# Order of a put-off channel's two products beside the last mixing

## The chip, the cores and the metric

The kernel runs on one core of one Trainium2 chip. The metric is the device time of one execution in microseconds (us); less is better. Before the change the median of three runs is 2989.25 us (2988.33 to 2990.84).

## The reference

The input is x, 4 images of 64 channels of 256 x 256 values in float32. Four layers follow each other.

```python
# layers 0, 1 and 3: a long convolution per channel
k   = einsum('ijk,imk->ijmk', hx, hy)[0]        # rank one per channel: hx along rows, hy along columns
y   = irfft2(rfft2(x, 512x512) * rfft2(k, 512x512))[..., :256, :256]
out = y + x * bias[:, None, None]

# layer 2: a Haar transform, a mixing of channels, and back
f1  = haar2d(x)
for i in range(2):
    f4  = einsum('bchw,oc->bohw', f1 * v[i], conv_w[i])
    acc = acc + sign(f4) * relu(abs(f4) - tau[i])
out = haar2d(acc, inverse=True) + x
```

hx and hy come from small networks with three sines each. The convolution's kernel of a channel is an outer product of one function of the row and one of the column, cut to the first 256 outputs, so the convolution is a product with a triangular Toeplitz matrix from each side.

## The kernel before, in words

**Products.** An image channel lies on chip as `[128, 2, 256]`: 128 partitions, two halves of the rows, 256 columns. One convolution is two products. `contract` (L186) makes one: four matmuls against a Toeplitz tile that was read from DRAM by `toeplitz` (L177). The four matmuls are eight records in the trace, since a float32 matmul is split in two. `first` (L192) makes the first product of a channel into a PSUM bank (`pa`), and ScalarE copies it to an SBUF tile (`a`, L198). `second` (L203) multiplies that tile into another bank (`py`), and VectorE adds bias times the channel's own input and writes the result (`y`, L211). So a channel's second product can't start until ScalarE has copied its first.

**Layers and stages.** For each image b, `convolutions(b)` does layers 0 and 1 and the forward Haar transform, and writes the coefficients to DRAM. `mixing(b)` (L310) then takes them in 64 groups g of four coefficient rows each: `load` (L314), `mix` (four matmuls, L334, into the bank pair `px`; then scaling of `px` to `f4`, ten of sixteen pieces on VectorE, L351, and six on ScalarE, L353, for the last image), `shrink` (abs and sign on ScalarE, L359 and L360, subtraction on VectorE, L361), `signed` (L366) and `add` (L370), which writes the tile `z`. `inverse(b)` (L377) reads `z` channel by channel: after `butterfly` come a copy (L387), row products (L394, L395, bank `pw`), a column product (L407, bank `pu`), the addition of the kept input (L411, L414, L415), giving `u`; then layer 3 with `first`, `second` and the store, which `last` (L430) lists.

**Put-off channels.** For images 0 to 2 every third channel (2, 5, ..., 62: 21 channels, 63 in all) stops at `u`, which goes to DRAM (`late`, L425). `convolution` (L437) takes these 63 up again and does layer 3 for them while the mixing of image 3 runs. Its stages per channel are: `load` (u and the Toeplitz tile through the SP queue, L444 and L180), `first`, `second` and the store (through ScalarE's queue, L434).

**The order.** Nothing is issued when a stage function is defined. `at(tick, place, run, unit)` (L227) collects events, and at the end they are sorted by tick, then place, then order of entry, and run. The mixing of image 3 gives group g, at tick start + g, place -1 to `mix`; -2 to `shrink` of the group before, -3 to `signed` of the one before that, and -4 to `add`. Loads have place 0, two ticks ahead. `convolution` gives each channel a tick; the 63 ticks are spread evenly by `spread` (L451) from start - 2 to two ticks behind the end of the mixing, so that some ticks have no channel. Its four stages get the four ticks from there on, with places 0, -1, -2, -3. `mixing` enters its events first, so at equal places its stage comes first. The framework below (a tile context) then orders the instructions of each engine itself, with this order as priority, gives out the buffers, and sets the waits.

**Buffers at this place.** The channel's u lies in the tag "in" (three buffers) from its load until `y` has been computed. The copy `a` has the tag "mid" (two buffers), the result `y` "co" (two), the Toeplitz tile "toep" (five). The four PSUM banks of tag "mm" take `pa`, `py`, `pw` and `pu`; two pairs of banks of tag "mix" take `px`. `f4` and `mag` have two buffers each.

The functions that the change touches, and what calls them:

Of the kernel before, what the change touches and what calls it, by code (L numbers as in the profile page):

```python
# [37 lines left out]
def conv_seq_kernel(ctx, tc, x, fz, fw, bias, decay, haar, haar_row, factors, vt, taut, wmix, out):  # L38
# [138 lines left out]
    def toeplitz(layer, c, name):  # L177

        t = tp.tile([P, 2, S], F32, name=name, tag="toep")
        nc.sync.dma_start(t, ap(pads[layer], c * 2 * ROW, [[1, P], [ROW, 2], [1, S]]))  # L180
        return t
# [10 lines left out]
    def first(b, st, key, layer, new):  # L192
        def run(c):
            s = st[c]
            ps = bank(f"p{new}_{b}_{c}")
            contract(ps, s[key], s[layer][:, 0, :])
            a = io.tile([P, 2, S], F32, name=f"{new}_{b}_{c}", tag="mid")
            nc.scalar.copy(a, ps)  # L198
            s[new] = a

        return run

    def second(b, st, key, layer, res, new, tag, ahead=None):  # L203
        def run(c):
            s = st[c]
            if ahead is not None:
                s[ahead] = toeplitz(ahead, c, f"t{ahead}_{b}_{c}")
            ps = bank(f"p{new}_{b}_{c}")
            contract(ps, s[key], s[layer][:, 1, :])
            y = io.tile([P, 2, S], F32, name=f"{new}_{b}_{c}", tag=tag, bufs=BUFS[tag])  # L210
            nc.vector.scalar_tensor_tensor(y, s[res], bsb[:, layer, c : c + 1], ps, ALU.mult, ALU.add)  # L211
            s[new] = y

        return run
# [12 lines left out]
    def at(tick, place, run, unit):  # L227
        events.append((tick, place, len(events), run, unit))
# [201 lines left out]
    def last(b, st):  # L430
        return [
            first(b, st, "u", 2, "a3"),
            second(b, st, "a3", 2, "u", "y3", "co"),
            lambda c: nc.scalar.dma_start(out[b, c].rearrange("(k p) w -> p k w", p=P), st.pop(c)["y3"]),  # L434
        ]

    def convolution(which, ticks):  # L437

        for (b, c), tick in zip(which, ticks):
            st = {}  # L440

            def load(c, b=b, st=st):
                u = io.tile([P, 2, S], F32, name=f"v_{b}_{c}", tag="in", bufs=3)
                nc.sync.dma_start(u, late[b, c])  # L444
                st[c] = {"u": u, 2: toeplitz(2, c, f"t2_{b}_{c}")}

            for s, stage in enumerate([load, *last(b, st)]):
                at(tick + s, -s, stage, c)


    def spread(begin, end, n=C):  # L451
# [23 lines left out]
    for b in range(B):  # L475
        mixing(b, start, 12 if b + 1 < B else 6)
        end = start + groups + 3
        if b + 1 < B:
            ready = convolutions(b + 1, spread(ahead, end + 2), in_parts=range(C), border=end)
        else:  # L480
            convolution(
                [(i, c) for i in range(B - 1) for c in sorted(put_off)], spread(start - 2, end + 2, (B - 1) * len(put_off))
            )
        inverse(b, end, put_off if b + 1 < B else ())

        start = max(end + C, ready + 3)
        ahead = start - 3
# [111 lines left out]
```

## Time and profile before

| what | value |
|---|---|
| median of 3 runs | 2989.25 us |
| profiled execution: its time, its span | 2989.2 us, 2987.4 us |
| granted TensorE clock | 1.00 |
| TensorE matmul busy | 2919.9 us (98%) |
| VectorE busy | 2551.9 us (85%) |
| ScalarE busy | 2156.5 us (72%) |
| first and last first product of a put-off channel (start) | 2444.3 us, 2743.5 us |
| first and last result y of a put-off channel (start) | 2450.9 us, 2748.1 us |
| put-off u, issue to landing, min / median / max | 2.6 / 3.7 / 5.8 us |

The profile is of one execution, whose own time is 1.8 us over the span from its first to its last instruction. Engines are PE (matmul), PEld (weight load), DVE (VectorE), ACT (ScalarE), and the queues SP and ACT that issue DMAs. In a timeline each row has its start, its length, the engine, the line of the kernel and the tiles written and read; a bracket tells how long the engine stood idle before it and what ended that. Times of start count from the span's start. Lengths of neighbouring VectorE instructions overlap, so the distance between two starts tells more than the length.

### The profile page before, as it was taken

Reading aid. Unit: us, or ns where it says so; the run is one execution under the profiler, and the core shown is the slowest. Engines: PE = TensorE matmul, PEld = TensorE weight load, DVE = VectorE, ACT = ScalarE, POOL = GpSimd, SP = SyncE. Lnnn points to the kernel's source line nnn. Section 1 sums busy time; section 2 is a strip of 40 time slices with the busy share of each in tenths; the row PEclk is TensorE's granted clock in tenths of the full one; section 3 lists DMA queues with packets and bytes.
Section 4 is the critical chain, followed back from the end, with each engine's and each line's share of the span. In section 5 each row is a group of like instructions: output and inputs, shape, how many; then the busy total and the mean of one; then the engine's idle time right before and its main releaser. Section 6 shows DMA issues by size and latency. Waiting matters only on the chain. (4 is left out here: it accounts for less than half of the span.)

```text
span 2987.4 us, 51999 instructions
## 1 busy us (share of the span) xinstructions
PE 2919.9 (98%) x16950; PEld 2610.5 (87%) x16950; DVE 2551.9 (85%) x4576; ACT 2156.5 (72%) x5005; POOL 0.2 (0%) x4
## 2 busy tenths in 40 slices
PE   7999999999999999999999999999999999999999
PEld 6899988888888888888888988888888988888998
DVE  4766778999998879999989879999998889998776
ACT  1333338999986758989886758989886768887554
POOL 0000000000000000000000000000000000000000
PEclk9999999999999999999999999999999999999999
DMA  4877777766667876676777776676677877777676
GB/s 146 245 234 229 230 231 210 210 200 199 210 201 243 249 219 203 207 209 203 208 213 236 253 224 196 209 211 204 206 211 235 255 238 231 231 232 220 212 210 187
DMA packets 562496, 649.72 MB, mean 217 GB/s; under 512 B 44369, under 2 KB 447412, under 8 KB 562100
## 3 DMA queue, kind: packets, MB, share of 16 engines
q1 hardware_dynamic: 446132, 494.94, 58.0%
q10 hardware_dynamic: 116096, 151.46, 14.2%
q8 instruction: 137, 2.24, 0.3%
q14 instruction: 131, 1.07, 0.1%
HBM read 426.77 MB, written 219.48 MB: 216 GB/s over the span
## 5 line engine op out<-in xcount | busy, mean ns | idle before, releaser
L189 PE MATMUL py<-t,a 128*128 128x256 f32 x3072 | 923.3, 382 | 17.8 <-ACT a L198 8.6
L198 ACT COPY a<-pa 128x512 f32<-128x512 f32 x768 | 473.3, 617 | 442.2 <-PE pa L190 298.2
L190 PEld LDWEIGHTS py<-t,a 128*128 128x128 f32 x3072 | 583.4, 190 | 79.3
L353 ACT ACTIVATE f<-px,vt 128x64 f32<-128x64 f32 x2688 | 589.7, 351 | 75.7 <-DVE f L351 75.3
L190 PE MATMUL py<-t,a 128*128 128x128 f32 x3072 | 590.0, 274 | 0.0
L189 PEld LDWEIGHTS py<-t,a 128*128 128x128 f32 x3072 | 491.6, 191 | 69.5 <-ACT a L198 32.0
L334 PE MATMUL px<-wb,f 128*128 128x256 f32 x2048 | 504.3, 382 | 19.6 <-ACT f L353 19.6
L334 PEld LDWEIGHTS px<-wb,f 128*128 128x128 f32 x2048 | 362.1, 190 | 67.2 <-ACT f L353 32.1
L361 DVE TENSOR_TENSOR mag<-mag,vt 128x1024 f32<-128x1024 f32 x256 | 312.7, 1222 | 18.8 <-ACT mag L359 16.6
L366 DVE SCALAR_TENSOR_TENSOR mag<-mag,f 128x1024 f32<-128x1024 f32 x256 | 312.8, 1222 | 4.4 <-DVE sd L266 0.3
L397 ACT CAST w<-pw 128x512 fp32r<-128x512 f32 x256 | 150.2, 587 | 226.5 <-PE pw L395 214.6
L189 PE MATMUL pa<-t,y 128*128 128x256 f32 x1024 | 306.6, 381 | 2.5 <-DVE y L211 1.6
L189 PE MATMUL pa<-t,x 128*128 128x256 f32 x1024 | 305.6, 380 | 1.5 <-issue 1.5
L359 ACT ACTIVATE mag<-f 128x1024 f32<-128x1024 f32 x256 | 282.9, 1105 | 21.1 <-DVE z L370 7.0
L387 ACT COPY zc<-z 128x512 f32<-128x512 f32 x256 | 282.4, 1104 | 2.3 <-ACT w L397 1.9
L360 ACT ACTIVATE f<-f 128x1024 f32<-128x1024 f32 x256 | 273.2, 1067 | 13.1 <-DVE sd L257 5.7
L278 DVE TENSOR_TENSOR sp<-sd,sp 128x512 fp32r<-128x512 f32 x256 | 176.6, 690 | 92.6 <-ACT sp L277 91.9
L211 DVE SCALAR_TENSOR_TENSOR y<-x,bsb,py 128x512 f32<-128x512 f32 x256 | 191.0, 746 | 55.5 <-PE py L190 48.7
L189 PE MATMUL pa<-t,u 128*128 128x256 f32 x772 | 232.8, 383 | 3.6 <-PE pu L407 3.5
L411 DVE SCALAR_TENSOR_TENSOR t<-r,pu 128x512 f32<-128x512 f32 x256 | 175.0, 684 | 59.4 <-PE pu L407 55.2
L190 PEld LDWEIGHTS pa<-t,x 128*128 128x128 f32 x1024 | 194.6, 190 | 26.3
L190 PEld LDWEIGHTS pa<-t,y 128*128 128x128 f32 x1024 | 194.5, 190 | 26.3
(65 smaller groups left out, 4471.6 us busy)
## 6 DMA issues: line engine op xcount, KB each, us to landing
t<-pad SPq DMA_DIRECT2D x768, 256.0 KB, 4.0
x<-in_x SPq DMA_DIRECT2D x256, 256.0 KB, 3.9
keep<-sd ACTq DMA_DIRECT2D x256, 256.0 KB, 2.9
coef<-co SPq DMA_DIRECT2D x256, 256.0 KB, 3.1
f<-coef SPq DMA_DIRECT2D x256, 256.0 KB, 4.0
r<-keep SPq DMA_DIRECT2D x256, 256.0 KB, 3.2
out_y<-y ACTq DMA_DIRECT2D x256, 256.0 KB, 3.7
late<-u ACTq DMA_DIRECT2D x63, 256.0 KB, 2.8
```

Of the source, the lines that this page charges most:

```text
L189: nc.tensor.matmul(ps[:, m, :], src[:, 0, m * P : (m + 1) * P], t[:, ::-1], start=True, stop=False)
L190: nc.tensor.matmul(ps[:, m, P:], src[:, 1, m * P : (m + 1) * P], t[:, : P - 1 : -1], start=False, stop=True)
L198: nc.scalar.copy(a, ps)
L211: nc.vector.scalar_tensor_tensor(y, s[res], bsb[:, layer, c : c + 1], ps, ALU.mult, ALU.add)
L278: nc.vector.tensor_tensor(w[:, 1], t, w[:, 0].bitcast(F32), ALU.subtract)
L334: nc.tensor.matmul(ps[:, h, q, :], f[:, q, h * P : (h + 1) * P], wb.rearrange("p r n -> p (r n)"), start=True, stop=True,)
L353: nc.scalar.mul(f4[:, j], px[:, j], scale(g, 0)[:, j : j + 1])
L359: nc.scalar.activation(mag, f4, AF.Abs)
L360: nc.scalar.activation(f4, f4, AF.Sign)
L361: nc.vector.tensor_sub(mag, mag, over(g, 1, 16))
L366: nc.vector.scalar_tensor_tensor(mag, mag, 0.0, st[g]["f4"], ALU.max, ALU.mult)
L387: nc.scalar.copy(a, z[:, :, :, c].rearrange("p h (i k) -> p h k i", k=2))
```

## The change

The places of a put-off channel's stages are no longer 0, -1, -2, -3 but 0, -2, -1, -3. `load` and the store keep their places and all four keep their ticks. In a tick, the emitted order of what stands around `mix(g)` was: second(c-2), mix(g), first(c-1). It becomes: first(c-1), mix(g), second(c-2). No instruction, buffer or transfer is added or taken away.

```diff
@@ convolution @@
                 nc.sync.dma_start(u, late[b, c])
                 st[c] = {"u": u, 2: toeplitz(2, c, f"t2_{b}_{c}")}
 
-            for s, stage in enumerate([load, *last(b, st)]):
-                at(tick + s, -s, stage, c)
+
+            for s, (place, stage) in enumerate(zip((0, -2, -1, -3), [load, *last(b, st)])):
+                at(tick + s, place, stage, c)
```

## The prediction

> **What bounds the kernel now.** I began with the busy shares of the page, then went to the stretch that the change touches, from the first put-off product (2444 us) to the first row product of the last inverse (2739 us). The first line says only that TensorE is the engine to watch over the whole span:
>
> ```profile
> PE 2919.9 (98%) x16950; PEld 2610.5 (87%) x16950; DVE 2551.9 (85%) x4576; ACT 2156.5 (72%) x5005; POOL 0.2 (0%) x4
> ```
>
> The view by stretches has, in order: span of the stretch, PE, PEld, DVE, ACT and POOL busy, clock, DMA share, GB/s.
>
> ```profile
> 2640.00:2680.00 40.00, 39.29 (x211) 34.52 (x210) 39.71 (x47) 35.62 (x83) 0.00 (x0) 1.00 0.79 234
> 2680.00:2724.00 44.00, 43.28 (x236) 38.52 (x235) 43.80 (x52) 38.43 (x95) 0.00 (x0) 1.00 0.76 223
> 2724.00:2740.00 16.00, 12.44 (x73) 10.83 (x72) 12.16 (x17) 10.27 (x20) 0.00 (x0) 1.00 0.78 223
> 2740.00:2987.00 247.00, 243.40 (x1557) 224.22 (x1555) 174.75 (x322) 138.78 (x192) 0.00 (x0) 1.00 0.67 203
> ```
>
> See that in the mixing VectorE is as full as TensorE (the six stretches from 2480 to 2724 sum to 242.0 of 244 us). From 2740 on TensorE alone carries the time, one channel each 3.74 us. Only the 16 us between have slack on both.
>
> The timeline of VectorE shows why the order on that engine matters. Two cycles of one group plus one put-off channel (start, us, engine, line):
>
> ```profile
> 2707.00 1.22 DVE L366 SCALAR_TENSOR_TENSOR mag<-mag,f 128x1024 f32<-128x1024 f32 x1
> 2708.14 0.75 DVE L211 SCALAR_TENSOR_TENSOR y<-v,bsb,py 128x512 f32<-128x512 f32 x1
> 2708.80 0.82 DVE L351 TENSOR_TENSOR f<-px,vt 128x640 f32<-128x640 f32 x1
> 2709.53 1.22 DVE L361 TENSOR_TENSOR mag<-mag,vt 128x1024 f32<-128x1024 f32 x1
> 2710.66 0.69 DVE L370 TENSOR_TENSOR z<-mag 128x512 f32<-128x512 f32 x1
> 2711.26 1.22 DVE L366 SCALAR_TENSOR_TENSOR mag<-mag,f 128x1024 f32<-128x1024 f32 x1
> ...
> 2520.45 1.22 DVE L366 SCALAR_TENSOR_TENSOR mag<-mag,f 128x1024 f32<-128x1024 f32 x1
> 2521.78 0.82 DVE L351 TENSOR_TENSOR f<-px,vt 128x640 f32<-128x640 f32 x1
> 2522.52 0.74 DVE L211 SCALAR_TENSOR_TENSOR y<-v,bsb,py 128x512 f32<-128x512 f32 x1
> 2523.17 1.22 DVE L361 TENSOR_TENSOR mag<-mag,vt 128x1024 f32<-128x1024 f32 x1
> 2524.31 0.69 DVE L370 TENSOR_TENSOR z<-mag 128x512 f32<-128x512 f32 x1
> 2524.91 1.22 DVE L366 SCALAR_TENSOR_TENSOR mag<-mag,f 128x1024 f32<-128x1024 f32 x1
> ```
>
> With the channel's result y (L211) straight behind L366 the cycle is 2711.26 - 2707.00 = 4.26 us; with the scaling L351 there it is 2524.91 - 2520.45 = 4.46 us. L351 writes the buffer of f4 (two of them) that L366 has just read, so it starts 1.33 us after L366, where y starts 1.14 us after: 0.19 us lost. Read through from 2480 to 2728, 45 cycles have y straight behind L366 and 2 have L351, then y.
>
> Last, the waits of the matmul stream behind the mixing. Each is a second product (py) standing until the copy (L198) of its own first product is done:
>
> ```profile
> 2726.06 0.70 PE L189 MATMUL py<-t,a 128*128 128x256 f32 x2 [1.54 <-ACT a L198]
> 2729.62 0.70 PE L189 MATMUL py<-t,a 128*128 128x256 f32 x2 [0.67 <-ACT a L198]
> 2733.18 0.70 PE L189 MATMUL py<-t,a 128*128 128x256 f32 x2 [0.67 <-ACT a L198]
> 2736.74 0.70 PE L189 MATMUL py<-t,a 128*128 128x256 f32 x2 [0.67 <-ACT a L198]
> ```
>
> Within the mixing, waits of 2480 to 2724 give:
>
> ```profile
> PEld px L334 <- ACT f L353: 6.7, 12, 1.2
> PE px L334 <- ACT f L353: 4.3, 7, 0.8
> PEld py L189 <- ACT a L198: 4.1, 14, 0.4
> ```
>
> The upper two are back-pressure: TensorE is ahead of the scaling and has no free px.
>
> **What the Trainium skill says.** "Perfetto Trace Analysis", Identifying the Most-Contended Engine: matmul busy time misleads, pipelined PE work looks smaller. So I use start-to-start pitch: a mix is 1.73 us, a product (contract) 1.31 us. "TensorE: Matmul & The Clock Gate", Step-by-step: weights of the next matmul load while the present one runs. The trace agrees: a py that has waited shows 0.70 us for its first pair, others 0.60, so each wait costs 0.10 us more than its gap. "VectorE: DVE Perf Modes", The DRAIN you can't avoid: a next instruction waits for the pipe to empty, unless it is not held. Here instructions of 1.22 us are followed after 1.13 to 1.14 us when independent and after 1.33 when dependent; the measurement decides.
>
> **The change, part by part.** It adds and removes no instruction, byte or buffer; it changes where three stages of a put-off channel stand within a tick. The emitted order is not the engine's order: on TensorE at 2705 I read mix (6 records), py, mix (2), pa. It acts as a rank among ready work. The load and the store keep their ranks (0 and -3), so SP's u and Toeplitz loads and ACT's store keep their place among the mixing's loads and issues. Before: second(c-2), mix(g), first(c-1). After: first(c-1), mix(g), second(c-2). With first go its 4 matmuls (8 records) and ACT's copy, 0.59 us each; ACT has it ahead of mix's six scalings instead of behind. With second go 4 matmuls and VectorE's y, now ranked behind mix's L351.
>
> *TensorE, in the mixing.* Between first(c) and second(c) now stands at least another product or a mix (1.31 or 1.73 us), more than the copy (0.59 us, starting 0.17 us after pa). The 4.1 us of py waits go. But VectorE sets the pace there: group pitch is (2726.71 - 2454.06) / 63 = 4.33 us while TensorE needs 1.73 + 0.89 channels x 2.62 = 4.06. What TensorE gains turns into longer waits at px. Value 0; bounds -2 (VectorE's own stops in that stretch, at most) to 0.
>
> *TensorE, behind the mixing.* The gaps are 1.54 + 3 x 0.67 = 3.55 us; with 4 x 0.10 it is 3.95. If pa of the next channel fills them, 2.7 products come forward from behind 2740, where they cost full price. About 1.4 y of 0.66 us then stand in VectorE ahead of the last z and the butterfly, which release the inverse: 3.55 - 0.9 = -2.6 us. Bounds 0 (nothing ready) and -3.95.
>
> *VectorE.* y now ranks behind L351. Each cycle that turns from the first form to the second costs 0.19 us. If L351 isn't yet free at the end of L366 (its buffer is released only there) and y is ready, y still goes first. I take 8 of the 45: +1.5 us. Bounds 0 and 45 x 0.19 = +8.6.
>
> *Loads of u.* The ring of three "in" buffers is full: u's load at 2704.65 starts as y of 2703.88 ends. The product that uses the load of 2700.39 starts at 2707.04; landing takes 3.7 us (median; 2.6 to 5.8), so 2.95 us are left. Ranked ahead of py and the rest of a mix, pa moves 1.31 + 0.43 us forward: 1.2 us left. A median load stays hidden, the slowest would stand out by 0.9 us. Value 0; upper bound in the rivals. "mid" (2), "toep" (5) and the four product banks hold one channel more between first and second; I find no bound.
>
> *Start of the stretch.* Up to 2480, stops of VectorE sum to 4.6 us, mostly waits for py and px. Reordering may shift these either way: 0, bounds -4 and +2.
>
> **Sum:** -2.6 + 1.5 = -1.1 us against the profiled execution's 2989.2 us (span 2987.4 and 1.8 around it): 2988.1. The median shown is 2989.25, practically the same.
>
> **Rivals.**
> A (the forecast, 0.43): steady part untouched, tail partly recovered: 2988; own range 2984 to 2993.
> B (0.30), slower: y falls behind L351 in nearly all cycles. For it: new rank, and the 4.46 us form already exists. Against: at the end of L366 y was ready and L351 was just being released. 45 x 0.19 - 2.6 = +6.0: 2995; without the tail 2998. It loses from 14 turned cycles on; past 0.2% at 45.
> C (0.12), slower: longer-held u buffers. TensorE stands in order at pa for the load, px behind it is late, VectorE starves. The first 0.28 us per group are covered (4.33 - 4.06 rounded); at a mean wait of 0.5 us it is 63 x 0.22 = +14: 3003. Against: 1.2 us left at the median.
> D (0.15), faster: VectorE's 4.6 us at the start go as well as the tail: -2.6 - 4.6 = -7: 2982. Against: at the start TensorE is full, not waiting.
> That the edit does nothing lies in A.
>
> **How the numbers follow.** 0.2% (6 us) is about what a measurement of this kernel tells from no change. Slower: C and two thirds of B, plus a little of A: 0.33. Faster: D: 0.15. The rest, 0.52, is no change. The range leaves out most of C and the far end of D: 2981 to 3000. A alone would be 2984 to 2993.
>
> **What would show it.** Right: py no longer waits for a; the gaps from 2724 to 2740 shrink from 3.55 to about 1 us; the forms on VectorE stay mostly at 4.26 us. B: cycles at 4.46 us in the many, the first row product near 2748. C: new waits of pa for late or v. Wrong altogether: a change before 2440 us or a longer pitch than 3.74 us behind the mixing.

## The result, and the profile after

The changed kernel is slower: 3008.52 us median of four runs (3003.68 to 3011.66), against 2990.05 us for the kernel before, also of four. The ratio is 1.0062 with a 95% interval of 1.0050 to 1.0074. The forecast was 2988.1 us with a range of 2981 to 3000; the time lies outside it, on the side of rival C.

The profiled execution took 3011.05 us, its span is 3009.24 us, 21.9 us over that of before. Three marks tell where they lie (starts, read from the timelines):

| | last scaling on VectorE (L351) | first row product (L394) | end of span |
|---|---|---|---|
| before | 2726.71 | 2739.46 | 2987.37 |
| after | 2749.29 | 2758.79 | 3009.24 |
| difference in the part | mixing +22.6 | tail 9.50 for 12.75: -3.2 | inverse 250.4 for 247.9: +2.5 |

First the engines of the whole span. PE's busy time has grown by 3 us only, so nearly all of the new time is waiting:

```profile
PE 2923.0 (97%) x16950; PEld 2614.3 (87%) x16950; DVE 2553.6 (85%) x4576; ACT 2158.8 (72%) x5005; POOL 0.2 (0%) x4
```

By stretches (span, PE, PEld, DVE, ACT, POOL busy, clock, DMA share, GB/s), the mixing has lost on both engines. VectorE had 39.7 of 40 us in the first stretch before. In the third row TensorE stands still for most of the time, and its mean clock is 0.61:

```profile
2640.00:2680.00 40.00, 36.41 (x194) 31.93 (x193) 36.64 (x43) 31.90 (x79) 0.00 (x0) 1.00 0.75 214
2680.00:2724.00 44.00, 42.82 (x234) 38.19 (x233) 41.81 (x49) 36.40 (x86) 0.00 (x0) 1.00 0.83 239
2752.00:2762.00 10.00, 3.21 (x12) 2.94 (x13) 6.35 (x10) 6.57 (x11) 0.00 (x0) 0.61 0.27 83
```

The waits from 2480 to 2752 us (who waited, for whom, us in total, times, longest) name the new cause:

```profile
PE pa L189 <- DMA v<-late: 15.7, 18, 2.2
DVE y L211 <- PE py L190: 14.9, 21, 2.4
PEld pa L189 <- PE py L190: 9.6, 15, 1.1
...
PEld px L334 <- ACT f L353: 0.5, 2, 0.3
PEld py L189 <- ACT a L198: 0.3, 1, 0.3
```

The first product (pa) now waits for the load of its u, and VectorE's y for the second product behind it. The wait that the reordering was to remove, py for the copy a, has gone from 4.1 to 0.3 us. The back-pressure at px has gone from 6.7 to 0.5 us as well: TensorE is no longer ahead of VectorE, it is behind.

The chain of waits around 2700 us shows why the load is late (start, us, what):

```profile
2686.45 4.15 DMA v<-late
...
2694.01 0.43 PE py L189 x2
...
2695.36 0.76 DVE y L211
2696.12 0.02 issue
2696.14 3.91 DMA v<-late
2700.05 0.14 issue
2700.18 0.67 PE pa L189 x2
2700.85 1.73 PE px L334 x8
...
2704.76 1.73 PE px L334 x8
2706.49 0.63 PE pa L189 x2
...
2708.66 0.43 PE py L189 x2
2709.09 0.23 PE py L190 x2
2709.33 0.03 issue
2709.35 0.75 DVE y L211
```

and the SP queue's timeline the loads of u in it:

```profile
2690.88 0.32 SPq L444 DMA_DIRECT2D v<-late  x1
...
2696.14 0.32 SPq L444 DMA_DIRECT2D v<-late  x1
...
2700.48 0.32 SPq L444 DMA_DIRECT2D v<-late  x1
...
2705.58 0.32 SPq L444 DMA_DIRECT2D v<-late  x1
...
2710.13 0.32 SPq L444 DMA_DIRECT2D v<-late  x1
```

With three buffers, the load of 2710.13 takes the buffer of the load of 2696.14. One lap is 13.99 us: load and its signal 4.04, the channel's first product with a mix inside it 3.27 (until 2703.45), the second product of the channel in front 1.31, the next mix 1.73, the **next** channel's first product 1.51, the own second product 1.33, y with its signals 0.80. Nothing in this sum is slack. A third of it is 4.66 us per channel, more than VectorE's 4.26. The 40 commonest VectorE cycles of the changed kernel have a mean of 4.76 us.

The chain holds a second loop, and it is as tight. It passes through TensorE's order, not through one buffer. The first product that waits for the load of 2686.45 holds up the second product behind it (2694.01), which is that of the channel in front. Its y (2695.36) frees the buffer for the load of 2696.14. With 2690.88 between them, these are two loads in 9.69 us, or 4.85 us per channel.

The lap in the old order is read from the trace of before:

```profile
2700.39 0.32 SPq L444 DMA_DIRECT2D v<-late  x1
...
2707.04 0.59 PE L189 MATMUL pa<-t,v 128*128 128x256 f32 x2
...
2712.40 0.75 DVE L211 SCALAR_TENSOR_TENSOR y<-v,bsb,py 128x512 f32<-128x512 f32 x1
2713.17 0.32 SPq L444 DMA_DIRECT2D v<-late  x1
```

From load to load that is 12.78 us or three VectorE cycles. With the median landing time of 3.7 us it holds 2.95 us of slack ahead of the first product, and some 1.4 us ahead of y.

The tail, in TensorE's timeline:

```profile
2758.79 0.79 PE L394 MATMUL pw<-hrow,zc 128*128 128x128 f32 x2 [7.38 <-ACT zc L387]
2759.38 0.42 PE L395 MATMUL pw<-hrow,zc 128*128 128x128 f32 x1
2759.59 0.64 PE L394 MATMUL pw<-hrow,zc 128*128 128x128 f32 x2
2760.02 0.42 PE L395 MATMUL pw<-hrow,zc 128*128 128x128 f32 x1
2760.23 1.06 PE L189 MATMUL py<-t,a 128*128 128x256 f32 x2
```

The four waits of before are gone, but one of 7.38 us has come. In TensorE's order the program before has nine products between the last mix and the first row product, the changed one has four (most of the first of them stands behind the mix that it encloses). A second product that is long ready (2760.23) stands behind the row product, which waits for z. The matmuls that follow run at about half speed (0.64 us for what takes 0.39 in the trace of before) until about 2764.

### The profile page after: what moved, and what is told of

Same layout as the page of the kernel before. It is cut to its first block, busy times and chain, and to the rows that moved or that the text cites. A ratio compares the mean times of both kernels' runs of the same rounds, so it can differ in the third digit from the quotient of the medians.

```text
span 3009.2 us, 52033 instructions
## 1 busy us (share of the span) xinstructions
PE 2923.0 (97%) x16950; PEld 2614.3 (87%) x16950; DVE 2553.6 (85%) x4576; ACT 2158.8 (72%) x5005; POOL 0.2 (0%) x4
## 4 chain that ended last, share of the span: by engine, by line
PE 61%; DVE 23%; ACT 6%; DMA 6%; issue 3%; DVEq 0%; ACTq 0%; SPq 0%
PE py L189 15%; PE pa L189 14%; PE py L190 7%; PE pa L190 7%; PE px L334 6%; DVE y L211 5%; DVE mag L366 4%; DVE mag L361 4%; PE pu L407 4%; PE pw L394 4%; ACT f L353 4%; DMA v<-late 2%; DMA keep<-sd 2%; PE pz L285 2%; DVE sd L267 2%
## 5 line engine op out<-in xcount | busy, mean ns | idle before, releaser
L334 PE MATMUL px<-wb,f 128*128 128x256 f32 x2048 | 498.1, 381 | 16.4 <-ACT f L353 16.4
L366 DVE SCALAR_TENSOR_TENSOR mag<-mag,f 128x1024 f32<-128x1024 f32 x256 | 312.4, 1220 | 5.0 <-ACT f L360 0.5
```

Source lines behind the costliest of these rows:

```text
L334: nc.tensor.matmul(ps[:, h, q, :], f[:, q, h * P : (h + 1) * P], wb.rearrange("p r n -> p (r n)"), start=True, stop=True,)
L366: nc.vector.scalar_tensor_tensor(mag, mag, 0.0, st[g]["f4"], ALU.max, ALU.mult)
```

## The experiments

The theory: the new order holds each u for one more channel, so three buffers are too few. The expectations call it the ring theory, a ring being a set of buffers that is used in turn. The rivals: the ranks themselves (the order or rank theory) break the pace of VectorE or of the mix; or the load itself is late, whatever holds the buffer.

**Three slots elsewhere, then four, then eight.** u goes to slots of the tile `sd`, which no other stage uses beside the last mixing, in place of the tag "in". Only the number of slots differs, and the last of the four has the old order.

```diff
-        for (b, c), tick in zip(which, ticks):
+        for i, ((b, c), tick) in enumerate(zip(which, ticks)):
...
-            def load(c, b=b, st=st):
-                u = io.tile([P, 2, S], F32, name=f"v_{b}_{c}", tag="in", bufs=3)
+            def load(c, b=b, st=st, i=i):
+                u = sd[:, i % N].rearrange("p k e w -> p k (e w)")
```

N = 3:

> The new order, the put-off u in three slots of the tile sd, which is idle beside the last mixing, in place of the three buffers of tag 'in'. Ring theory (three buffers for u are too few for the new order): the number is the same, so as slow as the changed kernel, 3004 to 3012 us. If the place in memory or the shared tag matters, it moves by more than 6 us.

Measured 3006.37 us, ratio 1.0059 (1.0044 to 1.0074). As slow as the changed kernel: neither the place nor the shared tag matters. In its waits from 2480 to 2745 stands the same line as above:

```profile
PE pa L189 <- DMA sd<-late: 10.4, 17, 1.5
```

N = 4:

> The new order with four slots. Ring theory: the lap of a buffer in the changed kernel's trace is about 14.0 us, which four slots share as 3.5 us per channel, under the 4.26 us that VectorE needs; the waits of pa for the load go from some 38 us to under 5 and the time to 2984 to 2990 us. Order theory (the ranks themselves break the pace of VectorE or ScalarE, whatever the buffers): within 4 us of the three-slot kernel.

Measured 2986.54 us, 0.9993 (0.9984 to 1.0002). One more slot takes away the whole loss of some 20 us; no wait of pa for a load is left in the list. The 38 us of the expectation was too high: the rows PE and PEld of pa's waits count in part the same time. In the timeline of the changed kernel's TensorE, the gaps ahead of pa (start to start, over the usual distance) sum to 26 us.

N = 8:

> The new order with eight slots. Ring theory: no more than four slots already give, so within 3 us of a_sd4; the copies' two 'mid' buffers limit what is left. If the time falls on by more than 3 us, four slots were still a limit.

Measured 2987.69 us, 0.9994 (0.9985 to 1.0002): no more than four slots give.

N = 8 in the old order:

> The old order with eight slots, the control. Ring theory: in the old order a load landed 2.95 us before its product, so more slots give nothing: 2987 to 2992 us. If more slots help the old order as well, by over 4 us, the ring was a limit of the kernel before and not brought by the change.

Measured 2988.53 us, 1.0000 (0.9991 to 1.0009). The ring was no limit in the kernel before; the edit has made it one.

**Which half of the edit.** Both keep the three buffers.

```diff
-zip((0, -2, -1, -3), [load, *last(b, st)])
+zip((0, -1.5, -2, -3), [load, *last(b, st)])    # o_first_up: second, first, mix
+zip((0, -0.5, -1, -3), [load, *last(b, st)])    # o_second_down: mix, second, first
```

> One half of the edit alone, with the three 'in' buffers: first(c-1) ahead of mix(g), second(c-2) still ahead of first(c-1). Ring theory: u is held no longer than before, since no other channel's product stands between its own two for longer, so 2984 to 2993 us. Rank theory (products ahead of the mix starve VectorE): 3000 us or more.

Measured 2984.79 us, 0.9989 (0.9982 to 0.9996).

> The other half alone, with the three 'in' buffers: second(c-2) behind mix(g), but still ahead of first(c-1). Ring theory: as before, 2984 to 2993 us. Rank theory (y behind L351, or the second product too late): 3000 us or more.

Measured 2985.62 us, 0.9995 (0.9986 to 1.0003).

Each half by itself costs nothing; the first is even a little faster than the kernel before, by 3 us. So it isn't the rank of a product against the mix. It is the crossing of the two halves: only where first(c-1) stands ahead of second(c-2) is u held for one more channel.

**Freeing u early.** The order of the changed kernel and its three "in" buffers, but y takes a slot of `sd`, which doesn't change here, instead of u. This leaves out the own bias term of the 63 channels.

```diff
-    def last(b, st):
+    def last(b, st, res="u"):
...
-            second(b, st, "a3", 2, "u", "y3", "co"),
+            second(b, st, "a3", 2, res, "y3", "co"),
...
-                st[c] = {"u": u, 2: toeplitz(2, c, f"t2_{b}_{c}")}
+                st[c] = {"u": u, "k": sd[:, 0].rearrange("p k e w -> p k (e w)"), 2: toeplitz(2, c, f"t2_{b}_{c}")}
...
-            for s, (place, stage) in enumerate(zip((0, -2, -1, -3), [load, *last(b, st)])):
+            for s, (place, stage) in enumerate(zip((0, -2, -1, -3), [load, *last(b, st, "k")])):
```

> The new order in full with the three 'in' buffers, but the bias term of the 63 put-off channels takes a constant tile in place of u (their own bias term is left out), so u is free after its first product and no longer held until y. Ring theory: the lap falls from some 14 us to load + first product, about 6 us, and the time to that of four slots, 2983 to 2990 us. If it is the load itself or its issue that is late, whatever holds the buffer, it stays over 3000 us.

Measured 2985.53 us, 0.9991 (0.9983 to 1.0000). The same loads, in the same order, with three buffers, are in time once y no longer holds them. This excludes the load's own duration and its issue as the cause.

**Two slots in the old order.** N = 2 in the edit above, in the kernel before.

> The old order with only two slots for u. Ring theory: the least lap of the old order is about load 3.9 + first product 1.3 + part of a mix 1.3 + second product 1.3 + y 0.75 = 8.6 us, so two slots give 4.3 us per channel, just at what VectorE needs: waits of pa for the load appear, and the time rises, but less than in the changed kernel (14.0/3 = 4.7 us): 2990 to 3003 us. If the old order doesn't depend on the slots at all, it stays within 3 us of before.

Measured 3011.30 us, 1.0078 (1.0061 to 1.0095): the same illness without the edit, and more of it than I had expected. The commonest VectorE cycle (33 of them) has a mean of 4.78 us (4.27 to 7.50), so two channels take 9.6 us where I had summed a least lap of 8.6; what makes up the difference was not followed further. The wait is the same:

```profile
PE pa L189 <- DMA sd<-late: 10.9, 13, 2.0
```

**What the four slots leave.** With the ring cured the new order is equal to the old one, not better. Its trace (a_sd4) has the tail's wait in full:

```profile
2738.46 0.80 PE L394 MATMUL pw<-hrow,zc 128*128 128x128 f32 x2 [9.81 <-ACT zc L387]
```

The channels run so far ahead that only the end of one second product, a first and a second are left behind the last mix; they end at 2728.6. Yet one first and two second products still stand behind the first row product. A narrower spread, from four ticks later to three ticks earlier, should bring more products between the two:

```diff
-[(i, c) for i in range(B - 1) for c in sorted(put_off)], spread(start - 2, end + 2, (B - 1) * len(put_off))
+[(i, c) for i in range(B - 1) for c in sorted(put_off)], spread(start + 2, end - 1, (B - 1) * len(put_off))
```

> The new order with four slots, and the 63 ticks spread from start + 2 to end - 1 in place of start - 2 to end + 2, so that three more products stand between the last mix and the first row product. Tail theory (with four slots TensorE stands 10 us at the first row product because the order has put nothing in front of it): that wait falls to about 6 us, no half-clock matmuls follow or fewer, and the time falls from 2986.5 to 2979 to 2984 us. If the mixing gets longer by what the tail saves, it stays at 2985 to 2989 us.

Measured 2982.85 us, 0.9979 (0.9971 to 0.9987): 6 us faster than the kernel before, clear of noise, and the fastest version here. The wait at the first row product is down to 2.45 us, further than expected, and the matmuls behind it are at full speed after their first pair (0.39 us):

```profile
2733.17 0.49 PE L394 MATMUL pw<-hrow,zc 128*128 128x128 f32 x2 [2.45 <-ACT zc L387]
2733.50 0.27 PE L395 MATMUL pw<-hrow,zc 128*128 128x128 f32 x1
2733.61 0.39 PE L394 MATMUL pw<-hrow,zc 128*128 128x128 f32 x2
```

The wait isn't all of the gain, though. By the marks of its trace the mixing is as long as before (274.1 us from the first group's L345 to the last L351; before 274.0). The tail takes 10.94 us for 12.75, the inverse 246.9 for 247.9, with no put-off product left in it. The mixing also starts 4.5 us earlier (2448.1 for 2452.7): the first put-off product now starts at 2458.4, behind that start, where before a first and a second product stood ahead of it. Starts of 2449 to 2453 in other versions with the old spread show that part of this differs from run to run; the shares were not separated.

From 2480 to 2720 us TensorE has no gap left, and a mix starts every 4.35 us, its own work with a channel in every tick (1.73 + 2 x 1.31).

Two controls with the same spread. The old order with its three buffers:

> The old order and three 'in' buffers, with the same later spread, the control for a_sd4_late. If the spread by itself is worth something, 2980 to 2986 us; if a denser row of channels, one in nearly each tick, costs what the tail saves, 2986 to 2993 us.

Measured 2987.87 us, 0.9994 (0.9985 to 1.0002). And the half edit:

> First product ahead of the mix, second ahead of first, three 'in' buffers, and the later spread. If the gain of o_first_up (3 us) and of the spread add up, 2977 to 2983 us; if both are the same few waits behind the mixing, 2982 to 2986 us.

Measured 2986.49 us, 0.9993 (0.9987 to 1.0000). The gains don't add up; it is no faster than without the spread, and half a microsecond over the second case. Of the three versions tried, the narrower spread pays only with the new order and four slots. In b_late the reason can be read from VectorE, whose timeline shows L351 straight behind L366 in 58 cycles at a mean of 4.45 us:

```profile
2693.20 1.22 DVE L366 SCALAR_TENSOR_TENSOR mag<-mag,f 128x1024 f32<-128x1024 f32 x1
2694.52 0.82 DVE L351 TENSOR_TENSOR f<-px,vt 128x640 f32<-128x640 f32 x1
2695.26 1.22 DVE L361 TENSOR_TENSOR mag<-mag,vt 128x1024 f32<-128x1024 f32 x1
2696.39 0.74 DVE L211 SCALAR_TENSOR_TENSOR y<-v,bsb,py 128x512 f32<-128x512 f32 x1
2697.05 0.69 DVE L370 TENSOR_TENSOR z<-mag 128x512 f32<-128x512 f32 x1
2697.65 1.22 DVE L366 SCALAR_TENSOR_TENSOR mag<-mag,f 128x1024 f32<-128x1024 f32 x1
```

This is the form that rival B had feared for the changed kernel, at its price. In o_first_up_late many of VectorE's cycles have two y (19, mean 4.98 us) or none (17, mean 3.87 us). Two such cycles take 4.43 us each on the mean, over the 4.26 us of a cycle with one y. What brings two y together was not followed further.

## Why the prediction was wrong

*What bounds the mixing.* Right on the average: VectorE at 4.26 us per cycle with TensorE close behind. The 4.06 us for TensorE, though, are a mean over ticks with and without a channel; in a tick with one TensorE needs 1.73 + 2 x 1.31 = 4.35 us, more than VectorE. It gets its lead in the ticks without a channel, where it needs 1.73 us and VectorE 3.80 (six cycles of before). a_sd4 comes back to the old time in it within 4 us (last L351 at 2730.52), and no frequent cycle with a channel in it is shorter than 4.26 us in any version here.

*The waits of py.* Right as a mechanism: 4.1 us in the mixing became 0.3, and the four gaps of the tail are gone. That this would gain nothing in the mixing was right too, as a_sd4 shows.

*The tail, -2.6 us.* The part is 3.2 us shorter, but not as I described; that the numbers are close is luck. No products came forward into it. Five of its nine were already done, and one wait of 7.38 us took the place of four that summed to 3.55. It cost 2.5 us more behind it, through the clock, which was in no term of mine.

*VectorE, +1.5 us.* The price was right (b_late), the number of cycles was not needed: 50 of the changed kernel's cycles still have y straight behind L366. Rival B did not happen. What made them long is y waiting for py (14.9 us).

*Loads of u, value 0.* This is the step that failed. I moved pa 1.74 us forward against a load that I left where it was, and found 1.2 us of slack. But the load starts when y of the channel three places ahead is done, and y moved back: between a channel's two products stood most of a mix (six of its eight records), and now stand the second product of the channel in front, a whole mix and the next channel's first product. The quantity to work out was the whole lap, load to load, against three times the cycle: 14.0 us against 12.8. It gives 13.99 / 3 - 4.26 = 0.40 us per channel, some 25 us over 63 channels; the mixing grew by 22.6. This sum was made afterwards, and it leaves out the ticks without a channel, in which the ring can catch up, and the second loop. I wrote of "mid", "toep" and the product banks that they would hold one channel more, and named the longer-held u in rival C, but did not put a number on how much longer it is held.

*Start of the stretch, 0.* From 2444 to 2480 us VectorE was busy for 26.7 us, before for 28.8. Its stops there did not go, so rival D did not happen.

*Rival C* had the mechanism, place and sign right, at a chance of 0.12 and 3003 us, and the range left it out. It assumed that 0.28 us of wait per group would be covered by TensorE's slack (4.33 - 4.06 is 0.27). The gaps ahead of pa are 26 us or 0.41 per group, and 0.36 per group was lost (0.30 against a_sd4, which has the same order), so little was covered: the lap runs through VectorE's y and through the in-order TensorE, and the mix behind the waiting pa is late with it.

## What to carry to other kernels

A reorder within a software pipeline changes how long each buffer is held; write down the lap of every ring that it stretches (load, all that stands between, last reader, next load), divide by the number of buffers, and compare with the pace of the bound engine, before pricing any wait that it removes. Look also for loops that pass from one unit to the next through an in-order engine: here two loads shared 9.69 us, although there were three buffers. Each load that starts just as the last reader of its buffer ends marks a ring without a spare buffer: it will take the pace as soon as its slack is used up. Where work fills a gap in front of a dependent stage, count what is left for the gap after the change; work done earlier leaves it empty.

## What the runs showed of the hardware

I had not expected that one wait of TensorE would slow the matmuls behind it. After 7.38 us (after) and 9.81 us (a_sd4) without a matmul, pairs of row products took 0.64 us in place of 0.39, for about 5 us, and the inverse took 250 us from its first row product in place of 248. With the same wait of 9.8 us in a_sd8 and a_early_free, the slow stretch was about 3 us and the inverse 249 us. After 2.45 us (a_sd4_late) no such stretch followed. The Trainium skill, "TensorE: Matmul & The Clock Gate", What's actually happening, states that the array's clock is halved after an idle window of about 3.4 us and freed after as long a busy one; the gaps fit that, though none lies near enough to the limit to test it, and the slow stretches of 3 to 5 us are near its figure for the way back.
